# Two attention blocks on one core: every q, k and projection product by quarters, summed in PSUM

## The chip, the cores and the metric

The kernel runs on one core of a Trainium2 chip. The metric is the device time of one launch in microseconds, the median of several runs. TensorE is the engine for matmuls (PE in the profile, PEld its weight loads), VectorE is DVE, ScalarE is ACT, GpSimd is POOL, and SP is the queue from which the transfers are issued.

## The reference

Two layers of self-attention over an image, each with a group norm ahead and a residual sum after it. x has 8 images of 512 channels and 32 x 32 = 1024 tokens, in float32. The layers differ in the group size of the norm and in their weights.

```python
xn = group_norm(x) * gamma + beta
q, k, v = split(einsum('oc,bcn->bon', qkv_w, xn) + qkv_b)   # 8 heads of 64
attn = softmax(einsum('bhdi,bhdj->bhij', q, k) / 8)
out = einsum('bhij,bhdj->bhdi', attn, v)
y = einsum('oc,bcn->bon', proj_w, out) + proj_b + x          # x of the next layer
```

## The kernel before

The work is cut into 16 units (layer, image), one after the other; the result of a unit's first layer goes through HBM (`mid`). In one unit there are four matrix products of 512x512 weights with a 512x1024 input: q, k, v from the normalized x (`xn`), and the projection (`o`) of the attention result (`ao`). Then comes attention. The projection of unit u is done in unit u+1, after that unit's q, k and v, so that it fills TensorE while the softmax's last sums are finished. The order of instructions on every engine is written out by hand; `done`, `rest` and the hooks below hang small work of the other engines behind a given product.

**Products by blocks.** A 512-wide product is cut into 2x2 blocks and done with seven block products instead of eight. Left factors are sums of weight blocks, right factors are sums of input blocks (`mix_weights`, `mix_right`). They are numbered 1 to 7, issued in the order 1, 6, 2, 7, 5, 4, 3, and each result block is a sum of several of them: 1+2; 1+6+5+3; 1+6+7+4; 1+6+7+5. One block product is done in one of two ways:

- whole (`block_product`, L416): four matmuls of 128x128 by 128x512, or eight by 128x256 where the result has tokens in rows (v). The profile counts two records for each float32 matmul.
- by quarters (`inner_products`, L455): the same seven-product scheme once more inside the block, seven matmuls of 128x128 by 128x256. Products 1, 6, 7 and 5 of the seven are copied out of PSUM by ScalarE into SBUF (L460), GpSimd adds them up (`fold`, L468 and L469) and onto the result (`rests`, L647 to L650 and L745).

By quarters go, from the second unit on, q's block products 2, 5, 4, 3, k's 1, 2, 7, 5, 4, 3 and the projection's 2, 3, 4; never v's, and none in the first unit:

```python
INNER = {"q": (2, 5, 4, 3), "k": (1, 2, 7, 5, 4, 3), "o": (2, 3, 4)}
```

PSUM has four pairs of banks, `s0`, `s1`, `a0`, `a1`. Block sums are formed by VectorE from PSUM and an SBUF tile (`p1`, `u2`, `u3` are the partial sums 1, 1+6, 1+6+7). The extra left factors of the quarters (three of 128x128 for each block) are made once per layer, kept in HBM (`inner_left`) and reloaded per unit; the weights themselves stay in SBUF.

**Attention** is 64 steps of two heads each. In a step TensorE makes scores (four matmuls of 64x64 by 64x512, L820) and, one or two steps behind, the product of the exponentials with v (L848). ScalarE takes the exponential into a buffer `p` of `ppool` (four of them, L828), VectorE adds up the softmax sums (L865, L867). `ppool` also holds the residual tiles of the projection. Within the steps the norm of the next unit's x, its right factors and the division by the softmax sums are done. Behind the last step come the last sums (`transposed`, `reduced`) and, in the next unit's first products, `reciprocals`, `divide` (L930) and `bias_last` (L937).

Of the kernel before, what the change touches and what calls it, by code (L numbers as in the profile page):

```python
# [18 lines left out]
P = 128  # L19
# [13 lines left out]
def fast_path(ctx, tc, x, qkv_wT, proj_wT, vecs, groups, out, flag):  # L33
# [5 lines left out]

# [11 lines left out]

    INNER = {"q": (2, 5, 4, 3), "k": (1, 2, 7, 5, 4, 3), "o": (2, 3, 4)}
    assert D == H and C == FD

    def pool(name, bufs, **kw):
# [4 lines left out]
    xnpool = pool("xnpool", 1)  # L69
    aopool = pool("aopool", 1)  # L70
    vpool = pool("vpool", 1)
    qkpool = pool("qkpool", CC)
    ppool = pool("ppool", 4)
    accpool = pool("accpool", 2)
    tpool = pool("tpool", 1)
# [8 lines left out]

# [3 lines left out]

    turns = [t[:, i, :] for i in range(2) for t in (*sbank, *apair)]

    vec = const.tile([P, 2, 6, CC], F32, name="vec")
    gmat = const.tile([P, 2, P], F32, name="gmat")
# [5 lines left out]
    inner_left = [  # L98
        {
            sel: mids.tile([P, len(ks), 3, P], F32, tag=f"il{sel}{l}", name=f"il{sel}{l}")  # L100
            for sel, ks in INNER.items()
# [6 lines left out]

    def gate(*insts):


        n = nc.tensor.nop(nofuse=True)
        n = getattr(n, "ins", n)
        for i in insts:
            tc.add_manual_dep(n, name_of(i), DEP, reason="tiles of the PE run independently")

    def load_x(u, tiles, first=0):
        l, b = units[u]
        src = x[b] if l == 0 else mid[b]
        for c, t in enumerate(tiles, first):  # L120
            nc.sync.dma_start(t, src[c * P : (c + 1) * P, :])

    def load_xn(u):
        t = xnpool.tile([P, CC, N], F32, tag="xn", name=f"xn_{u}")
        load_x(u, [t[:, c, :] for c in range(CC)])
        return t

    def load_res(u):
        tiles = [ppool.tile([P, N], F32, tag="p", name=f"x_{u}_{c}") for c in range(CC)]
        load_x(u, tiles)  # L130
        return tiles

    def load_weights(l, which=range(3), after=None):

        mats = []
        src = qkv_wT[l].rearrange("(c p) o -> p c o", p=P)
        for i in which:
            a = wpool.tile([P, CC, C], F32, tag=f"w{i}", name=f"w{i}_{l}")
            n = nc.sync.dma_start(a, src[:, :, i * C : (i + 1) * C])
            if after is not None:  # L140
                tc.add_manual_dep(
                    getattr(n, "ins", n), name_of(after), DEP, reason="x comes first"
                )
                after = None
            mats.append(a)
        return mats

    def mix_weights(l, mats, engine, first=0):


        lefts, parts = [], []
        add, sub = engine.tensor_add, engine.tensor_sub
        for i, a in enumerate(mats, first):
            a11, a12 = a[:, :2, :FD2], a[:, 2:, :FD2]
            a21, a22 = a[:, :2, FD2:], a[:, 2:, FD2:]
            s1, s2, s4 = (
                wpool.tile([P, 2, FD2], F32, tag=f"s{k}w{i}", name=f"s{k}w{i}_{l}")
                for k in (1, 2, 4)
            )
            parts += [  # L160
                partial(add, s1, a21, a22), partial(sub, s2, s1, a11),
                partial(sub, a21, a11, a21), partial(sub, s4, a12, s2),
            ]
            lefts.append({1: a11, 2: a12, 3: s4, 4: a22, 5: s1, 6: s2, 7: a21})
        return lefts, parts

    def mix_right(name, low, high):


        b11, b12 = low[:, :, :FD], low[:, :, FD:]  # L170
        b21, b22 = high[:, :, :FD], high[:, :, FD:]
        factors = {1: b11, 2: b21, 3: b22, 7: b12}

        def part(i):
            if i == 0:
                for k, n in ((5, 1), (6, 2), (4, 4)):
                    factors[k] = tpool.tile([P, 2, FD], F32, tag=f"{name[0]}{n}", name=f"{name}_t{n}")
            t1, t2, t4 = (factors[k] for k in (5, 6, 4))
            nc.vector.tensor_sub(
                *((t1, b12, b11), (t2, b22, t1), (t4, b21, t2), (b12, b22, b12))[i]  # L180
            )

        return factors, [partial(part, i) for i in range(4)]

    def mix_inner(b, t, engine):


        b11, b12 = b[:, 0, :FD2], b[:, 0, FD2:]
        b21, b22 = b[:, 1, :FD2], b[:, 1, FD2:]
        t1, t2, t3, t4 = (t[:, i, :] for i in range(4))  # L190
        sub = engine.tensor_sub
        return {1: b11, 2: b21, 3: b22, 4: t4, 5: t1, 6: t2, 7: t3}, [
            partial(sub, t1, b12, b11), partial(sub, t2, b22, t1),
            partial(sub, t3, b22, b12), partial(sub, t4, b21, t2),
        ]

    def inner_lefts(k, left, made):
        a11, a12 = left[:, 0, :P], left[:, 1, :P]
        a21, a22 = left[:, 0, P:], left[:, 1, P:]
        s1, s2, s4 = made  # L200
        return {1: a11, 2: a12, 3: s4, 4: a22, 5: s1, 6: s2, 7: a21}

    def mix_inner_in(b, t, engine):

        sub = engine.tensor_sub
        b11, b12 = b[:, 0, :FD2], b[:, 0, FD2:]
        b21, b22 = b[:, 1, :FD2], b[:, 1, FD2:]
        t1, t2, t4 = (t[:, i, :] for i in range(3))
        sub(t1, b12, b11)
        sub(t2, b22, t1)  # L210
        sub(b12, b22, b12)
        sub(t4, b21, t2)
        return {1: b11, 2: b21, 3: b22, 4: t4, 5: t1, 6: t2, 7: b12}

    def mix_inner_left(l, lefts):

        def part(sel, n, k, room, later=None, engine=nc.gpsimd):  # L220
            sub = engine.tensor_sub
            left = lefts[sel][k]
            s1, s2, s4 = room
            a11, a12 = left[:, 0, :P], left[:, 1, :P]
            a21, a22 = left[:, 0, P:], left[:, 1, P:]
            engine.tensor_add(s1, a21, a22)
            sub(s2, s1, a11)
            sub(a21, a11, a21)
            sub(s4, a12, s2)

            def out():
                for j in range(3):
                    nc.sync.dma_start(inner_left[l][sel][:, n, j, :], room[j])

            if later is None:
                out()
            else:
                later.append(out)

        return [partial(part, sel, n, k) for sel in lefts for n, k in enumerate(INNER[sel])]  # L240

    def left_rooms(name, pool, tag, cols):

        t = pool.tile([P, cols], F32, tag=tag, name=name)
        slices = [t[:, i : i + P] for i in range(0, cols, P)]
        return [slices[i : i + 3] for i in range(0, len(slices) - 2, 3)]

    def load_inner_left(u):

        l, _ = units[u]  # L250
        flat = vpool.tile([P, NT, C], F32, tag="v", name=f"il_{u}").rearrange("p t o -> p (t o)")
        made, end = {}, 0
        for sel in "qk":
            ks = INNER[sel]
            first, end = end, end + len(ks) * 3 * P
            part = flat[:, first:end].rearrange("p (k s o) -> p k s o", s=3, o=P)
            nc.sync.dma_start(part, inner_left[l][sel])
            made[sel] = {k: [part[:, j, i, :] for i in range(3)] for j, k in enumerate(ks)}
        return made

    def load_proj(l, tag):
        w = wpool.tile([P, CC, C], F32, tag=tag, name=f"wproj_{l}_{tag}")
        nc.sync.dma_start(w, proj_wT[l].rearrange("(c p) o -> p c o", p=P))
        return w

    def norm_parts(u, xs, lo=0, hi=CC):


        l, _ = units[u]
# [6 lines left out]
        def stats(c, h):  # L276
            if c == lo and h == 0:
                st["stats"] = small.tile([P, CC, NH, 6], F32, tag="stats", name=f"stats_{u}_{lo}")
                st["mv"] = small.tile([P, CC, 2], F32, tag="mv", name=f"mv_{u}_{lo}")[:, :n, :]
            st["last"] = nc.vector.bn_stats(st["stats"][:, c - lo, h, :], xs[:, c, ts(h, FD)])  # L280
# [34 lines left out]

# [16 lines left out]
        def apply(c, h):  # L332
            cols = xs[:, c, ts(h, FD)]
            nc.scalar.activation(  # L334
                cols, cols, AF.Identity,
                bias=st["shift"][:, c - lo : c - lo + 1], scale=st["scale"][:, c - lo : c - lo + 1],
            )

        def apply_now(c, h):
            cols = xs[:, c, ts(h, FD)]  # L340
# [7 lines left out]
    def norm_first(xs, weights, mixing):  # L348

# [4 lines left out]
        ) = (norm_parts(0, xs, lo, lo + 2) for lo in (0, 2))  # L357
# [7 lines left out]
        idle_products(3, xs[:, 0, :])  # L365
# [24 lines left out]
        def rest():  # L390
            variances_2(bank)
            mixing[0]()
# [4 lines left out]
            mixing[1]()  # L397
# [7 lines left out]
    def block_product(bank, a, b, tokens, start, stop, between=None):  # L405
        for i in range(4 if tokens else 2):
            if i == 1 and between is not None:
                between()
# [13 lines left out]
    def blocks(name, left, right, tokens, c11, others, done, u3_in, summed, inner={}, rests=None,  # L422
               u2_in=(trpool, "tr"), between=None, behind=None, p1=None):

# [1056 lines left out]
```

## Time and profile before

| | |
|---|---|
| median of 3 runs | 3257.65 us (3257.36, 3257.65, 3259.85) |
| span of the profiled execution, the only time listed for it | 3256.9 us |
| mean granted clock of TensorE | 0.999 |
| moved by DMA | 192.51 MB, 59 GB/s |

One unit in stages (the fourth), busy microseconds of each engine:

| stage | from, to (us) | length | PE | DVE | ACT | POOL |
|---|---|---|---|---|---|---|
| q | 600.4, 622.8 | 22.4 | 22.4 | 19.8 | 9.6 | 17.7 |
| k | 622.8, 644.6 | 21.8 | 21.8 | 14.9 | 9.3 | 21.5 |
| v | 644.6, 668.8 | 24.2 | 24.2 | 12.9 | 3.6 | 21.3 |
| projection of the unit before | 668.8, 691.7 | 22.9 | 22.9 | 20.8 | 5.1 | 7.1 |
| attention | 691.7, 802.0 | 110.3 | 110.3 | 100.7 | 76.9 | 10.5 |

The span is the time from the first to the last instruction. A run's time also has what lies around it: the median is 0.75 us above the span. A line of the profile names the source line, engine, operation, output and inputs with their shapes, and the number of instructions; in a timeline the first two numbers are start and length in microseconds. The ends of matmuls are modelled, so that a busy PE says that it has work, not that it runs at its peak; the distance from start to start shows its pace.

### The profile page before, as it was taken

Reading aid. Unit: us, or ns where it says so; the run is one execution under the profiler, and the core shown is the slowest. Engines: PE = TensorE matmul, PEld = TensorE weight load, DVE = VectorE, ACT = ScalarE, POOL = GpSimd, SP = SyncE. Lnnn points to the kernel's source line nnn. Section 1 sums busy time; section 2 is a strip of 40 time slices with the busy share of each in tenths; the row PEclk is TensorE's granted clock in tenths of the full one; section 3 lists DMA queues with packets and bytes.
Section 4 is the critical chain, followed back from the end, with each engine's and each line's share of the span. In section 5 each row is a group of like instructions: output and inputs, shape, how many; then the busy total and the mean of one; then the engine's idle time right before and its main releaser. Section 6 shows DMA issues by size and latency. Waiting matters only on the chain.

```text
span 3256.9 us, 56805 instructions
## 1 busy us (share of the span) xinstructions
PE 3244.5 (100%) x22206; PEld 1863.3 (57%) x22206; DVE 2715.3 (83%) x3488; ACT 1650.2 (51%) x2296; POOL 1216.3 (37%) x1207
## 2 busy tenths in 40 slices
PE   9999999999999999999999999999999999999999
PEld 5465474654746547465574655747556474564743
DVE  5887978789787897989979889797897978979786
ACT  1653626546274463744637446373563735637354
POOL 2054171531706317063270732607126071350710
PEclk9999999999999999999999999999999999999999
DMA  3112120121201212023120121201212012120111
GB/s 104 48 45 79 46 79 28 45 79 46 85 22 45 85 43 86 18 71 114 55 87 27 45 86 46 85 16 45 86 46 85 17 54 76 46 85 22 67 71 48
DMA packets 86463, 192.51 MB, mean 59 GB/s; under 512 B 22960, under 2 KB 34992, under 8 KB 84272
## 3 DMA queue, kind: packets, MB, share of 16 engines
q1 hardware_dynamic: 86192, 188.82, 17.0%
q8 instruction: 180, 2.95, 0.4%
q14 instruction: 91, 0.75, 0.1%
HBM read 148.00 MB, written 39.19 MB: 57 GB/s over the span
## 4 chain that ended last, share of the span: by engine, by line
PE 96%; DVE 3%; issue 0%; DMA 0%; ACT 0%; SPq 0%; DVEq 0%
PE a L848 26%; PE s L820 25%; PE s L416 14%; PE a L416 12%; PE a L455 10%; PE s L455 9%; DVE acc L867 1%; PE a L820 1%; PE s L766 0%; PE a L766 0%; DVE tr L880 0%; PE s L361 0%; DVE acc L865 0%; DVE ao L874 0%; DMA xn<-x_dram 0%
## 5 line engine op out<-in xcount | busy, mean ns | idle before, releaser
L828 ACT ACTIVATE p<-s 128x1024 f32<-128x1024 f32 x976 | 998.0, 1024 | 558.0 <-PE s L820 516.6
L848 PE MATMUL a<-p,v 64*64 64x512 f32 x8192 | 1099.8, 589 | 0.0
L820 PE MATMUL s<-q,k 64*64 64x512 f32 x7808 | 1058.1, 590 | 0.0
L867 DVE TENSOR_TENSOR acc<-acc,p 128x1024 f32<-128x1024 f32 x768 | 968.6, 1261 | 61.7 <-ACT p L828 13.0
L848 PEld LDWEIGHTS a<-p,v 64*64 64x64 f32 x8192 | 383.2, 131 | 495.8 <-ACT p L828 350.2
L820 PEld LDWEIGHTS s<-q,k 64*64 64x64 f32 x7808 | 383.5, 133 | 431.9 <-issue 422.8
L1088 POOL TENSOR_TENSOR r<-xn 128x256 f32<-128x256 f32 x30 | 49.5, 1649 | 1175.7 <-DVE acc L867 1038.3
L650 POOL TENSOR_TENSOR k<-k,m_k 128x512 f32<-128x512 f32 x180 | 259.6, 1463 | 0.0
L865 DVE TENSOR_TENSOR acc<-p,p 128x1024 f32<-128x1024 f32 x128 | 156.2, 1220 | 20.5 <-ACT p L828 13.9
L312 POOL TENSOR_TENSOR y<-var,half 128x4 f32<-128x4 f32 (+1 forms) x17 | 33.2, 1950 | 344.4 <-DVE var L310 344.4
L880 DVE STREAM_TRANSPOSE tr<-acc 128x1024 f32<-128x1024 f32 x128 | 157.9, 1234 | 0.0
L650 POOL TENSOR_TENSOR q<-q,m_q 128x512 f32<-128x512 f32 x120 | 157.2, 1325 | 0.0
L890 DVE TENSOR_REDUCE red<-tr 128x32 f32<-128x1024 f32 x128 | 154.4, 1206 | 0.6
L538 DVE TENSOR_TENSOR u_v<-s,p_v 128x1024 f32<-128x1024 f32 x32 | 39.2, 1224 | 123.7 <-PE s L416 123.7
L501 ACT COPY p_o<-a 128x1024 f32<-128x1024 f32 x15 | 15.2, 1012 | 244.2 <-PE a L416 244.2
L874 DVE TENSOR_TENSOR ao<-a,tmp 128x512 f32<-128x512 f32 x128 | 88.0, 688 | 60.9 <-ACT tmp L873 59.6
L460 ACT COPY m_q<-s 128x256 f32<-128x256 f32 x150 | 55.9, 373 | 145.3 <-PE s L455 142.7
L468 POOL TENSOR_TENSOR m_o<-m_o 128x256 f32<-128x256 f32 x45 | 34.2, 760 | 251.7 <-ACT m_o L460 251.7
L416 PE MATMUL s<-x_t,s2w 128*128 128x512 f32 x256 | 117.5, 592 | 0.0
L416 PE MATMUL a<-w,xn 128*128 128x256 f32 x496 | 112.1, 379 | 0.0
L460 ACT COPY m_k<-s 128x256 f32<-128x256 f32 x165 | 61.5, 373 | 93.8 <-PE s L455 90.2
L334 ACT ACTIVATE xn<-xn,shift,scale 128x512 f32<-128x512 f32 x124 | 99.5, 804 | 10.9 <-DVE shift L330 10.9
(291 smaller groups left out, 5130.5 us busy)
## 6 DMA issues: line engine op xcount, KB each, us to landing
rb<-drec SPq DMA_DIRECT2D x128, 256.0 KB, 3.9
xn<-mid SPq DMA_DIRECT2D x36, 512.0 KB, 7.9
il<-ilk SPq DMA_DIRECT2D x15, 1152.0 KB, 7.0
xn<-x_dram SPq DMA_DIRECT2D x32, 512.0 KB, 7.0
x<-x_dram SPq DMA_DIRECT2D x32, 512.0 KB, 5.5
x<-mid SPq DMA_DIRECT2D x28, 512.0 KB, 4.9
il<-ilq SPq DMA_DIRECT2D x15, 768.0 KB, 4.2
mid<-u_o SPq DMA_DIRECT2D x32, 256.0 KB, 2.1
```

What stands on the lines that cost most here:

```text
L334: nc.scalar.activation(cols, cols, AF.Identity, bias=st["shift"][:, c - lo : c - lo + 1], scale=st["scale"][:, c - lo : c - lo + 1],)
L416: nc.tensor.matmul(dst, at[:, c, ts(i, P)], moving[:, c, :], start=start and c == 0 and not (tokens and i % 2), stop=stop and c == 1, skip ...
L455: nc.tensor.matmul(dst[j], a[j], b[j], start=j in (1, 5) or first and j in (2, 4), stop=j not in (1, 6), skip_group_check=True,)
L460: taken.append(nc.scalar.copy(to[j], dst[j]))
L650: w.last[sel].append(add(cols, cols, rest[:, i, :]))
L820: nc.tensor.matmul(bank[e * H : (e + 1) * H, j, :], w.k[pr][j * H : (j + 1) * H, t * P + e * H : t * P + (e + 1) * H], w.q[pr][j * H : (j ...
L828: exp = nc.scalar.activation(p, bank, AF.Exp, scale=SCALE)
L848: nc.tensor.matmul(banks[r][j * H : (j + 1) * H, :], w.v[rows, t, lo : lo + D], p[rows, j, :], start=(t == 0), stop=(t == NT - 1),)
L865: nc.vector.tensor_add(acc, state["first"], p)
L867: nc.vector.tensor_add(acc, acc, p)
L880: nc.vector.transpose(tr, state["acc"].pop(c))
L890: nc.vector.tensor_reduce(red[:, :, qh, :], state["tr"].rearrange("p j (f i) -> p j f i", i=BL), AX.X, ALU.add)
```

## The change

- **All** block products of q, k and projection go by quarters, in every unit; only q's and k's product 1 of the first unit stay whole (`behind`). v stays whole.
- The quarter sums stay in PSUM. Each product has a main pair (`a0` or `a1`) and one pair for help (`s1` or `s0`), taken in turns by `Stream`. Quarter product 1 goes to a helper bank; ScalarE copies it into the main pair as a **seed** (for 1+2); 6 is added to it in the helper bank, copied again (for 1+6+4), then 5, copied twice (for 1+6+5+3 and 1+6+5). Products 2, 4 and 3 are added onto the seeds by TensorE. Product 7 goes to the helper pair's other bank and by ScalarE into an SBUF tile **`late`** (three buffers), which GpSimd adds to the lower half of the result after VectorE has read it (`add_late`). GpSimd's folding goes.
- The end of each product (quarter products 4 and 3) is issued behind the first matmul of the next (`tail`, `close`), in the last one behind the first scores.
- Order of a unit: v, q, k, projection. x's quarter factors are made by GpSimd in v, 16 subtractions. The projection's are made by VectorE in q and k.
- Left factors with their quarter factors are "images" in HBM, seven parts per layer and matrix (896 columns each, v 512); two slots in SBUF receive them product by product: q's and v's during attention, k's and the projection's from the end of v on, 28 loads per unit. First-layer images are made in the first unit, the others by VectorE in the attention of units 0 to 4 (`MAKE`).
- The residual tiles `res` (four, 512 KB each) are loaded during k and projection, and take three of `ppool`'s five buffers at its end, as one is used twice. The residual is added by VectorE at its own pass.

```diff
-    INNER = {"q": (2, 5, 4, 3), "k": (1, 2, 7, 5, 4, 3), "o": (2, 3, 4)}
+    ORDER = (1, 6, 2, 7, 5, 4, 3)
...
-    ppool = pool("ppool", 4)
+    ppool = pool("ppool", 5)
+    latepool = pool("latepool", 3)
...
+        def product(self, a, b, keep, finish):
+            i = self.n % 2
+            self.n += 1
+            main, aux, m, s = apair[i], sbank[1 - i], f"a{i}", f"s{1 - i}"
+            one, seventh = aux[:, 0, :FD2], aux[:, 1, :FD2]
+            q11, q12, q21, q22 = (main[:, r, ts(h, FD2)] for r in range(2) for h in range(2))
...
+            part(1, one, s, 0, True)
+            seed(q11, 0)
+            self.close()
+            part(6, one, s, 0)
+            seed(q21, 1)
+            part(2, q11, m, 0)
+            part(7, seventh, s, 1, not keep)
+            late = latepool.tile([P, FD2], F32, tag="late", name=f"late_{self.n}")
+            on("ACT", nc.scalar.copy(late, seventh), s, 1)
+            part(5, one, s, 0)
+            seed(q12, 0)
+            def tail():
+                part(4, q21, m, 1)
+                seed(q22, 1)
+                part(3, q12, m, 0)
+                finish(main, m, late)
+            self.tail = tail
...
+    def add_late(t, late):
+        cols = in_two(t[:, 1, :])
+        return nc.gpsimd.tensor_add(cols, cols, twice(late))
...
+        def u2(main, m, late):
+            t = st["u2"] = accpool.tile([P, 2, FD], F32, tag="acc", name=f"u2_{name}")
+            on("DVE", nc.vector.tensor_add(t, main, st["p1"]), m, 0, 1)
+            add_late(t, late)
...
+        def fifth(main, m, late):
+            wide(main, m)
+            result(1, 1, "u3")(main, m, late)
...
+        def third(*args):
+            take(0, 1, *args)
+            more(1, 0, "u3")
+            store(1, 0)
+            more(0, 1, "u2")
+            store(0, 1)
...
+    MAKE = {0: (0, "o"), 1: (1, "v"), 2: (1, "q"), 3: (1, "k"), 4: (1, "o")}
...
+            at("q", 1, partial(o_rooms, True), partial(ro.mix, 3))
+            at("q", 6, partial(ro.mix, 2))
+            at("q", 2, o_part((5, 6), 0, 1))
+            at("q", 7, o_part((5, 6), 2, 3))
+            at("q", 4, o_part((1, 7), 0, 1))
+            at("q", 3, o_part((1, 7), 2, 3))
+            at("k", 2, partial(o_rooms, False), o_part((4,), 0, 1, 2, 3))
+            at("k", 4, o_part((2, 3), 0, 1))
+            at("k", 3, o_part((2, 3), 2, 3))
...
+            at("q", 1, *(partial(load_image, l, "k", 0, k) for k in ORDER))
+            for k in ORDER:
+                at("q", k, partial(load_image, lo, "o", 1, k))
...
+            at("o", 3, partial(stats_of, 6, 7))
```

`at("q", 2, ...)` hangs work behind q's block product 2; an `o_part` step is one subtraction of 128x512 by VectorE. `fifth` is product 5, with two passes of VectorE over the main pair: `wide` adds it to `u2`, `result` adds `u3` to it. `third` is the projection's last product: `take` adds the main pair onto `res` and hangs `add_late` behind it, `more` adds a partial sum from SBUF.

## The prediction

> **What bounds the kernel now.** I read the busy times, then the chain, then TensorE's own waits, then its timeline.
>
> ```profile
> span 3256.9 us, 56805 instructions
> PE 3244.5 (100%) x22206; PEld 1863.3 (57%) x22206; DVE 2715.3 (83%) x3488; ACT 1650.2 (51%) x2296; POOL 1216.3 (37%) x1207
> PE 96%; DVE 3%; issue 0%; DMA 0%; ACT 0%; SPq 0%; DVEq 0%
> ```
> The end is set by TensorE (96% of the chain), and its four lines of waits over the whole span come to 5.9 us, 4.5 of them the first load. So TensorE is not merely busy: it has no gap. A change pays only by taking matmuls away, and every new wait is paid in full.
>
> The timeline of TensorE in one unit (start, us, instructions) prices the two kinds of product:
> ```profile
> 675.67 0.59 PE L455 MATMUL s<-ao,wproj_wproj 128*128 128x256 f32 x2
> ...
> 678.69 3.60 PE L416 MATMUL s<-ao,wproj_wproj 128*128 128x512 f32 x8
> 682.12 3.60 PE L416 MATMUL a<-o_t,s1w 128*128 128x512 f32 x8
> ```
> A product by quarters takes 678.69 - 675.67 = 3.02 us (seven matmuls, 0.4317 apart), a whole one 682.12 - 678.69 = 3.43. The gain is 0.41 each. The v product (16 records, 644.63 to 648.08) takes 3.45 and stays. A unit lasts 201.58 us (600.38 to 801.96).
>
> Next, the loop that a quarter product lives in, from the mixed timeline:
> ```profile
> 613.80 0.59 PE L455 MATMUL s<-x_t,s1w 128*128 128x256 f32 x2
> 614.44 0.37 ACT L460 COPY m_q<-s 128x256 f32<-128x256 f32 x1 [2.32 <-PE s L455]
> 614.92 0.37 PEld L455 LDWEIGHTS s<-r,il 128*128 128x128 f32 x2
> 615.10 0.59 PE L455 MATMUL s<-r,il 128*128 128x256 f32 x2
> ```
> The copy starts 0.64 after its matmul's start and ends at 614.81; the matmul that overwrites the copied bank loads its weights 0.11 later and starts 0.29 after that end. With two matmuls between (3 x 0.4317 = 1.295 us) the loop 0.64 + 0.37 + 0.29 = 1.30 just closes: that weight load came 0.46 after the one before instead of 0.43. Two matmuls hide a copy with nothing to spare.
>
> Last, VectorE beside GpSimd, from the same timeline:
> ```profile
> 622.73 1.02 DVE L636 TENSOR_TENSOR q<-a,u_q 128x512 f32<-128x512 f32 x2
> 623.39 1.26 POOL L650 TENSOR_TENSOR q<-q,m_q 128x512 f32<-128x512 f32 x1
> 623.67 1.27 DVE L578 TENSOR_TENSOR k<-xn 128x256 f32<-128x256 f32 x1
> 624.61 0.91 POOL L647 TENSOR_TENSOR q<-u_q,m_q 128x256 f32<-128x256 f32 x1
> 624.97 0.83 DVE L578 TENSOR_TENSOR k<-xn,k 128x256 f32<-128x256 f32 x1
> ```
> L636 reads PSUM (a) and is not slowed. L578 reads SBUF twice: 1.27 us where L209, the same shape with GpSimd idle, takes 0.43. It waited until GpSimd's addition was over, and then GpSimd's next one waited for it: they take turns.
>
> **What the Trainium skill says.** "SBUF — State Buffer", Who interferes with whom: an instruction of VectorE with two SBUF inputs and a GpSimd one that reads SBUF exclude each other for their whole length; with at most one SBUF input VectorE doesn't contend. The lines above agree (1.27 against 0.43). "PSUM — Partial Sum Buffer", PSUM bank collisions: accesses of two engines to one bank must be ordered even on different columns; hence the new copies wait by bank. No run here shows a collision. "ScalarE: Activation LUTs", Step-by-step: ScalarE's writes to PSUM have a lower latency than to SBUF; no copy of before writes PSUM, so no trace here shows it.
>
> **The change part by part.**
>
> *Removed from TensorE.* Of q, k and projection, 13 of 21 products per unit go by quarters now (4, 6, 3), all 21 afterwards: 8 x 15 units. In the first unit 12 of its 14 q and k products, none before. (120 + 12) x 0.41 = **54.1 us saved**.
>
> *Copies on ScalarE.* 4 per quarter product become 5 (four seeds within PSUM, one `late`): 780 become (15 x 21 + 12) x 5 = 1635, at 0.37 some 315 us more beside TensorE. Three seeds per product are on TensorE's path (after 1 for 6, after 6 for 5, after 5 for 3), each with two matmuls between. A seed of 0.37 or less costs nothing. Bounds: shorter gains nothing, as the loop is closed already; 0.03 longer costs 327 x 3 x 0.03 = 29 us. I take 0.
>
> *The main pair is reused two products later.* VectorE may start when product 3 is through and the last seed done: 9 x 0.4317 + 0.64, some 4.57 us after the product's first matmul. The seed of the next but one is due at 14 x 0.4317 + 0.64 = 6.68. About 2.1 us are left, 2.0 with a hand-over of 0.1. One pass over PSUM (128x1024, L538: 1.22) or two halves (1.41) fit; product 5 has two passes, 1.14 + 1.22 = 2.36 from start to end, so they end at 6.93, and the seed and with it matmul 6 come 0.25 late. That is three times per unit, twice in the first; q's is part of the next item, k's and projection's are 30 x 0.25 = 7.5, the first unit's 0.5.
>
> *VectorE's projection factors in q.* After q's products 2 and 7 two 128x512 subtractions from SBUF are queued behind the result, while GpSimd's `late` addition (1.25) becomes ready under the first. They alternate: 1.14 (result) + 0.61 + 1.2 (GpSimd) + 0.61 = 3.6 against a period of 3.02; then 1.32 + 0.61 + 1.2 + 0.61 = 3.7. Product 5 starts 0.6 + 0.7 = 1.3 late; 0.25 of its own is added, and about as much of slack was there before: **1.3 us per unit** (0.25 if VectorE goes twice running, 1.9 at the most), x 15 = 19.5.
>
> *Entry to attention.* The second scores take the bank of the last product's copies and must wait for its last seed: matmul 4 + 0.64 + 0.37 + 0.29 = 1.30 where 0.86 is free: 0.4 x 16 = 6.4. Behind the last product VectorE now has result, two additions into `res` (the second waits for GpSimd's 1.25) and two statistics before the first softmax sum: 1.14 + 1.14 + 1.3 + 1.14 + 1.2 = 5.9 us from 1.9 after the first scores. The sum ends 9.1 after them; before it started 3.2 after them (694.88 against 691.70). The fourth exponential needs that p buffer (`res` holds three of five); exponential 1.02 + 0.29 puts product 3 at 10.4, where 9.0 was due: **1.5 per unit** (0.5 without GpSimd in the way, 2.5 if the additions drag), x 15 = 22.5.
>
> *Mixing left factors in five units' attention.* Up to eight VectorE passes of 128x896, about 1.0 each by VectorE's rate in L538, in chunks of 13.7 us with 11.1 to 13.3 us busy in the stage view. The backlog is some 2 us at the end, and v's product 4 is late by most of it: it is due 17.27 after v's start and needs VectorE's pass over product 7, which I put at an end of 16.2 (the last softmax sum 3.3 after the stage's start as now, then evacuation, transposition, reduction, four passes and the reciprocals, 10.7, and some 2.2 of turns with GpSimd). 0.8 to spare, 1.6 x 5 units: 8 us (0 to 15).
>
> *Moved, at nothing.* v first: attention's last evacuation and v's sums have 3.45 per product. GpSimd's 16 subtractions of x (12 x 1.25 + 4 x 0.72 = 18 us) fit into v's 24, uncovered they would hold q's first matmuls. SP's queue gets 28 image loads per unit, 11.5 MB: k and projection 6.4 MB, free to start from v's middle; at the o stage's rate (212 GB/s at a share of 0.53, so 400 at full) 16 us, and k needs them only when q (21 us) is over. Behind them queue the reloads of x, due two to four products later. If they were late, each microsecond would be k's. The new opening (v, q, k first products instead of q, k, v) has the same three products before the first product 6: 0, within 2.
>
> Sum: -54.1 + 19.5 + 8.0 + 6.4 + 22.5 + 8 = **+10.3**. Against the profiled span of 3256.9 this is 3267.2; the runs' median is 0.75 above that span, which makes 3268.
>
> **Rivals.** *Alternation is mild (faster).* If VectorE gets its pair of subtractions through before GpSimd, product 5 in q costs 0.25 and the entry 0.4 + 0.5: 15 x 1.6 + 0.9 = 25, mixing 0: 3257.65 - 54.1 + 25 = 3229. For it: GpSimd's work halves, from 78 us per unit to about 40. Against it: the turns at 623 to 626. It decides once VectorE's second pass of q's product 5 ends within 2.0 us of being due.
> *Seeds in PSUM are slower.* 0.03 us over the closed loop, three times in 327 products: +29 on the forecast, 3297. For it: no spare in 614.44 to 615.10. Against: the skill's remark.
> *Everything hides.* 3257.65 - 54.1 = 3204. Against it: two passes in 2.0 us.
>
> **How the numbers follow.** Forecast 0.42 (own range 3250 to 3284), mild 0.33 (3212 to 3240), slow seeds 0.20 (3284 to 3315), all hidden 0.05. The range 3215 to 3305 leaves out all hidden, the low edge of mild and the top of slow seeds, under 0.2. A measurement can tell 0.2% (6.5 us) from no change: faster 0.38 (mild, hidden), same 0.15 (forecast's lower part), slower 0.47.
>
> **What would show it.** TensorE's waits should no longer be empty: matmuls on ScalarE's seeds, one of over 1 us per unit in q, about 0.25 in k and projection, one of about 1.5 on an exponential in the first steps of attention. The first softmax sum should start near 8 us after the first scores. q's subtractions should show 1 to 1.9 us instead of 0.69. Wrong it is if the sums of those waits are under 1.8 us a unit (mild), or if most products show three short waits (slow seeds), or if TensorE waits on DMA.

## The result and the profile after

The changed kernel takes 3298.94 us (median of 4 runs, 3297.93 to 3299.36), the kernel before 3257.77 in runs beside it: a ratio of 1.0125 (95% interval 1.0111 to 1.0139), 41 us slower. It lies within the stated range, but 31 us above the predicted time. The profiled execution has a span of 3296.1 us, 39.2 above the 3256.9 of before.

The page of the changed kernel, busy times and shares of the chain:

```profile
span 3296.1 us, 59529 instructions
PE 3221.7 (98%) x22998; PEld 2083.2 (63%) x22998; DVE 2900.7 (88%) x3298; ACT 1888.6 (57%) x3077; POOL 889.7 (27%) x559
PE 70%; DVE 21%; issue 5%; ACT 2%; DMA 1%; SPq 0%; POOL 0%; DVEq 0%; ACTq 0%
```

TensorE was all of the chain but 4%; now VectorE has a fifth of it. GpSimd's busy time fell by 327 us (from 1216.3), and yet, as the timelines further down show, GpSimd is what VectorE waits for. TensorE's waits over the whole span (who waited for whom: us in total, times, longest), 5.9 us before:

```profile
PE s L398 <- DVE u_v L625: 35.0, 15, 4.5
PE s L421 <- ACT a L426: 13.6, 16, 0.9
PE a L733 <- ACT p L713: 8.6, 6, 2.6
...
PE s L703 <- ACT a L426: 2.6, 16, 0.2
```

The second, third and last line are the forecast's: q's late seed, the exponential at the entry, the second scores. The first, the largest, was forecast only for five units, and for another product: it comes once in every unit after the first. L398 is v; the wait is that of v's fourth product in the order, 7, which is added onto the banks that VectorE's pass L625 (`u2`, the sum with product 6) must read first. TensorE's timeline at the start of an ordinary unit, the seventh (unit 6; units are counted from 0 below):

```profile
1240.31 3.62 PE L398 MATMUL a<-w,xn 128*128 128x256 f32 x16
1245.73 3.72 PE L398 MATMUL s<-w,xn 128*128 128x256 f32 x16 [1.81 <-DVE u_v L625]
```

Product 7 should start 3.45 after product 2, at 1243.76; it starts 1.97 later. VectorE's timeline ahead of it:

```profile
1228.13 1.22 DVE L217 TENSOR_TENSOR xt<-xn,xt 128x1024 f32<-128x1024 f32 x1
1229.26 2.29 DVE L752 TENSOR_TENSOR acc<-acc,p 128x1024 f32<-128x1024 f32 x1
1231.48 2.29 DVE L812 SCALAR_TENSOR_TENSOR ao<-ao,rb 128x1024 f32<-128x1024 f32 x1
...
1233.70 6.70 DVE L752 TENSOR_TENSOR acc<-acc,p 128x1024 f32<-128x1024 f32 x3
...
1242.19 1.22 DVE L772 TENSOR_REDUCE red<-tr 128x32 f32<-128x1024 f32 x1
1243.33 1.22 DVE L217 TENSOR_TENSOR xn<-xn 128x1024 f32<-128x1024 f32 x1
1244.46 1.22 DVE L625 TENSOR_TENSOR u_v<-s,p_v 128x1024 f32<-128x1024 f32 x1
```

Up to 1229 a pass of 128x1024 takes 1.22 (pace 1.13); the next five take 2.23 each (6.70 for three). Then GpSimd's timeline, same kernel:

```profile
1228.35 2.13 POOL L933 TENSOR_TENSOR xa<-xn 128x512 f32<-128x512 f32 x1 [77.48 <-PE s L703]
1230.55 2.14 POOL L933 TENSOR_TENSOR xa<-xn,xa 128x512 f32<-128x512 f32 x1
1232.77 2.14 POOL L933 TENSOR_TENSOR xb<-xn,xa 128x512 f32<-128x512 f32 x1
1234.86 2.25 POOL L933 TENSOR_TENSOR k<-xt 128x512 f32<-128x512 f32 x1
1237.19 4.34 POOL L933 TENSOR_TENSOR k<-xt,k 128x512 f32<-128x512 f32 x2
```

A piece alone takes 1.25, so these records include waiting. Start plus length gives their ends, and the ends of the two engines alternate: GpSimd 1230.48, VectorE 1231.55, GpSimd 1232.69, VectorE 1233.77. Each ends about one piece of work (1.1) after the other: turns, as in the prediction's lines at 623 to 626, but in a place where I had not looked for them. The six x pieces hang behind v's products 1 and 6, but nothing holds them until then: they start 5 us before v, under the last softmax sums. The same stretch of the kernel before:

```profile
595.23 1.22 DVE L179 TENSOR_TENSOR x_t<-xn,x_t 128x1024 f32<-128x1024 f32 x1
596.37 1.22 DVE L867 TENSOR_TENSOR acc<-acc,p 128x1024 f32<-128x1024 f32 x1
597.50 1.22 DVE L930 SCALAR_TENSOR_TENSOR ao<-ao,rb 128x1024 f32<-128x1024 f32 x1
...
598.64 5.08 DVE L867 TENSOR_TENSOR acc<-acc,p 128x1024 f32<-128x1024 f32 x3
...
605.51 1.22 DVE L890 TENSOR_REDUCE red<-tr 128x32 f32<-128x1024 f32 x1
```

There only three passes ran beside GpSimd, at 1.69 each, since its pieces were of 128x256. The reduction ended 11.5 us after the mixing line (L179) had started, in the changed kernel 15.3 (from L217 to the end of L772).

### The profile page after: what moved, and what is told of

The parts are those of the page before. It is cut to its first block, busy times and chain, and to the rows that moved or that the text cites. A ratio compares the mean times of both kernels' runs of the same rounds, so it can differ in the third digit from the quotient of the medians.

```text
span 3296.1 us, 59529 instructions
## 1 busy us (share of the span) xinstructions
PE 3221.7 (98%) x22998; PEld 2083.2 (63%) x22998; DVE 2900.7 (88%) x3298; ACT 1888.6 (57%) x3077; POOL 889.7 (27%) x559
## 4 chain that ended last, share of the span: by engine, by line
PE 70%; DVE 21%; issue 5%; ACT 2%; DMA 1%; SPq 0%; POOL 0%; DVEq 0%; ACTq 0%
PE s L703 18%; PE a L733 17%; PE s L421 17%; PE a L421 12%; DVE acc L752 9%; PE s L398 2%; PE a L398 2%; DVE tr L764 2%; DVE acc L750 2%; DVE ao L759 1%; ACT p L713 1%; DMA lt<-red 1%; DVE red L772 1%; DVE tot L793 1%; PE a L703 1%
## 5 line engine op out<-in xcount | busy, mean ns | idle before, releaser
L713 ACT ACTIVATE p<-s 128x1024 f32<-128x1024 f32 x976 | 1000.3, 1025 | 528.1 <-PE s L703 446.5
L426 ACT COPY a<-s 128x256 f32<-128x256 f32 x1308 | 463.3, 357 | 302.0 <-PE s L421 184.4
L438 ACT COPY late<-s 128x256 f32<-128x256 f32 x327 | 121.8, 373 | 178.7 <-PE s L421 178.7
L819 ACT ACTIVATE ao<-ao,vec 128x512 f32<-128x512 f32 x128 | 88.3, 714 | 221.9 <-DVE ao L812 221.9
L398 PE MATMUL a<-w,xn 128*128 128x256 f32 x768 | 178.2, 381 | 0.0
L398 PEld LDWEIGHTS a<-w,xn 128*128 128x128 f32 x768 | 144.4, 190 | 31.7 <-issue 12.2
L772 DVE TENSOR_REDUCE red<-tr 128x32 f32<-128x1024 f32 x128 | 154.2, 1205 | 0.6
L750 DVE TENSOR_TENSOR acc<-p,p 128x1024 f32<-128x1024 f32 x128 | 152.4, 1190 | 1.0 <-ACT p L713 1.0
L421 PE MATMUL s<-k,w 128*128 128x256 f32 x492 | 146.3, 379 | 0.0
L421 PE MATMUL a<-xn,w 128*128 128x256 f32 x492 | 146.3, 379 | 0.0
L421 PE MATMUL s<-xn,w 128*128 128x256 f32 x492 | 146.3, 379 | 0.0
L421 PE MATMUL a<-xt,w 128*128 128x256 f32 x462 | 139.0, 382 | 0.0
L421 PE MATMUL s<-xt,w 128*128 128x256 f32 x432 | 128.5, 379 | 0.0
L458 POOL TENSOR_TENSOR res<-res,late 128x512 f32<-128x512 f32 x60 | 103.6, 1726 | 88.4 <-DVE res L546 88.4
```

What stands on the lines that cost most here:

```text
L398: step()
L421: nc.tensor.matmul(dst, a[j], b[j], start=start, stop=j != 1, skip_group_check=True),
L426: n = nc.scalar.copy(dst, one)
L438: on("ACT", nc.scalar.copy(late, seventh), s, 1)
L458: return nc.gpsimd.tensor_add(cols, cols, twice(late))
L713: exp = nc.scalar.activation(p, bank, AF.Exp, scale=SCALE)
```

## The experiments

All were run beside the kernel before, whose median was 3258.1 and 3259.0 us in the two sets. The changed kernel was not run again in these sets; its 3299 us is taken from the section above. "Loss" is the distance between starts on TensorE beyond the usual one, from the trace; the "restart" is 0.10 us more between the first matmul after a wait and the next.

**GpSimd's pieces later.** The pieces that need VectorE's last mixing come first from the second unit on, so that GpSimd cannot start ahead of it (lines that stay the same are left out):

```diff
-        at("v", 1, make_rooms, partial(right.mix, 3), part_of((2, 3), 0, 1, 2))
...
-        at("v", 2, partial(right.mix, 2), part_of((1, 7), 0, 1, 2))
...
+        if u:
+            at("v", 1, make_rooms, partial(right.mix, 3), part_of((1, 7), 0, 1, 2))
...
+            at("v", 2, partial(right.mix, 2), part_of((2, 3), 0, 1, 2))
...
```

> From the second unit on GpSimd takes its x pieces in another order: the four that need v's last mixing of xn come first, so that GpSimd starts only when VectorE is through with the end of attention. Theory one (taking turns): in the changed kernel TensorE loses 2.45 us in v in ordinary units and some 5 in three others, 46 us in all, because VectorE's sums, each 1.14 us alone, last 2.2 beside GpSimd's subtractions. Without that VectorE's pass over v's product 6 ends 3.8 us earlier, before it is due: v loses under 0.4 us per unit and the kernel takes 3253 to 3265 us. Rival (VectorE simply has too much to do before that pass, since v is first now): the pass stays late, v loses over 1.5 us per unit, 3285 us or more. Second rival: GpSimd's pieces are late for q's first products, a new wait on GpSimd of over 1 us per unit.

Measured: 3252.87 us, ratio to before 0.9982 (0.9975 to 0.9989): 46 us off the changed kernel. Its VectorE timeline, same place of the same unit:

```profile
1216.36 1.22 DVE L772 TENSOR_REDUCE red<-tr 128x32 f32<-128x1024 f32 x1
1217.50 1.22 DVE L217 TENSOR_TENSOR xn<-xn 128x1024 f32<-128x1024 f32 x1
1219.73 1.22 DVE L625 TENSOR_TENSOR u_v<-s,p_v 128x1024 f32<-128x1024 f32 x1 [1.02 <-PE s L398]
```

v starts at 1212.45; VectorE is ready 6.3 us later and now waits for TensorE's product 6 itself. v's loss fell from 2.55 to 0.10 us in ordinary units. No new wait on GpSimd came instead, and the rival (VectorE has too much to do before that pass) is refuted. With this one reordering the change is 5 us faster than the kernel before.

**Smaller pieces in the old place.** Order unchanged, each piece of 128x512 made by two of 128x256:

```diff
-            sub = engine.tensor_sub
+            def sub(out, a, b):
+                n = out.shape[1] if engine is nc.gpsimd else 1
+                for i in range(n):
+                    at = slice(i, i + 1) if n > 1 else slice(None)
+                    engine.tensor_sub(out[:, at], a[:, at], b[:, at])
```

> GpSimd's x subtractions stay where they are, but each of 128x512 is made by two of 128x256: more instructions, the same data. If the two engines take whole turns, a sum of VectorE's waits for a piece half as long: 1.7 us each, as in the kernel before (5.08 us for three), where the changed kernel shows 2.23. Five such passes lie ahead of VectorE's pass over v's product 6, which then ends 2.7 us earlier: v's loss of 2.45 us per unit falls to under 0.5, and the kernel takes 3262 to 3272 us. If instead the two share a port evenly, the size of a piece changes nothing and the time stays at 3299.

Measured: 3257.09 us, ratio 0.9996 (0.9987 to 1.0005), 42 us off. VectorE's timeline:

```profile
1211.60 1.75 DVE L757 TENSOR_TENSOR acc<-acc,p 128x1024 f32<-128x1024 f32 x1
1213.27 1.75 DVE L817 SCALAR_TENSOR_TENSOR ao<-ao,rb 128x1024 f32<-128x1024 f32 x1
...
1214.95 5.07 DVE L757 TENSOR_TENSOR acc<-acc,p 128x1024 f32<-128x1024 f32 x3
```

1.69 each, as in the kernel before. GpSimd has the same data to go through in more instructions, and VectorE's five passes are 2.7 us sooner: each pays for about one GpSimd piece, long or short. By the expectation an even sharing of a port would have left 2.23. The pass of `u2` now ends 9.9 us after v's start, just ahead of its due time of 10.35, and v's loss is 0.10 us in ordinary units, under the 0.5 expected; hence the gain above the expected one.

**Fewer subtractions before product 5 of q.**

```diff
-            at("q", 7, o_part((5, 6), 2, 3))
+            at("k", 6, o_part((5, 6), 2, 3))
```

> Two of the four subtractions of projection factors that VectorE does behind q's product 7 are moved behind k's product 6. Theory (turns with GpSimd behind product 7 make product 5's two passes late): q's wait of 1.16 us per unit falls to k's and projection's 0.19, 15 us in all, 3284 us. Rival (product 5's two passes are late by themselves, or by the pair behind product 2): the wait stays over 0.8 us, 3294 us or more. Rival two: the pair is late for projection's product 6, or delays k's passes; then a new wait in k or projection takes the gain back.

Measured: 3286.48 us, ratio 1.0088 (1.0071 to 1.0105): 12.5 us off. In the changed kernel VectorE's second pass of product 5 came at 1277.93, behind the two subtractions (L990), of which the second is shown:

```profile
1275.12 1.75 DVE L990 TENSOR_TENSOR ot<-ot 128x512 f32<-128x512 f32 x1
1276.80 1.21 DVE L496 TENSOR_TENSOR u_q<-a,u_q 128x1024 f32<-128x1024 f32 x1
1277.93 1.21 DVE L509 TENSOR_TENSOR q<-a,u_q 128x1024 f32<-128x1024 f32 x1
```

The next seed came after it, and TensorE 1.06 late, as its timeline shows; the last line is behind the restart:

```profile
1278.15 0.59 PE L421 MATMUL a<-xt,w 128*128 128x256 f32 x2
1279.64 0.70 PE L421 MATMUL s<-xa,w 128*128 128x256 f32 x2 [0.90 <-ACT a L426]
1280.18 0.59 PE L421 MATMUL a<-xn,w 128*128 128x256 f32 x2
```

The same place with the edit:

```profile
1275.48 0.59 PE L421 MATMUL a<-xt,w 128*128 128x256 f32 x2
1276.00 0.70 PE L421 MATMUL s<-xa,w 128*128 128x256 f32 x2
1276.54 0.59 PE L421 MATMUL a<-xn,w 128*128 128x256 f32 x2
```

0.09 late plus a restart of 0.10, as in k and projection. The loss of q fell by 0.97 us per unit, 14.5 in all; some of it came back as longer waits in v (36.2 us in place of 35.0) and on the exponential (9.2 in place of 8.6). With the pair behind product 7 away, the pair behind product 2 costs nothing, as VectorE is then idle for 1.22 us ahead of product 5. While both stood it had a part: in the changed kernel VectorE goes from the first pair into product 7's pass at 1273.21 without a pause, some 0.5 after that product's last seed (1272.71), and from there into the second pair and product 5. So some 0.5 of the 1.16 may be the first pair's; moving that one alone was not tried.

**Raw loads later.** The raw left factors that units 0 to 4 mix are loaded at step 4 of attention, counted from 0, instead of before it.

```diff
-            load_raw(*make, left_slots[0])
...
+            if make is not None and s == 4:
+                load_raw(*make, left_slots[0])
```

> In the five units whose attention mixes a left factor the raw loads are issued at the fifth step of attention instead of ahead of its first. Theory (the loads share the DMA engines with the stores that the fourth exponential waits for: 5.7 us for a store of 256 KB there, 2.7 in other units): the wait of 1.4 us on the exponential goes in the units 1 to 4, 3293 us. Rival (the wait is VectorE's, the first softmax sum comes late): it stays, 3299 us. v's waits are unchanged in either.

Measured: 3294.17 us, ratio 1.0113 (1.0096 to 1.0129). The times alone don't tell 5 us from nothing, the trace does: the waits on the exponential (L713) fell from 8.6 us (6) to 3.9 (2). Those in units 1, 2, 4 and 14 are gone; the first unit's 2.6 stays, and so do 1.3 in unit 3. Unit 14 mixes nothing, so the 1.5 us there are not the edit's. ScalarE's timeline of the changed kernel at the entry of unit 2, from the third exponential on (the fourth and fifth are merged):

```profile
500.90 1.02 ACT L713 ACTIVATE p<-a 128x1024 f32<-128x1024 f32 x1
505.93 2.05 ACT L713 ACTIVATE p<-s 128x1024 f32<-128x1024 f32 x2 [4.01 <-DVE acc L750]
```

The same with the edit, third, fourth and fifth:

```profile
497.90 1.02 ACT L713 ACTIVATE p<-a 128x1024 f32<-128x1024 f32 x1
500.98 1.02 ACT L713 ACTIVATE p<-s 128x1024 f32<-128x1024 f32 x1 [2.07 <-DMA mid<-res]
502.92 1.03 ACT L713 ACTIVATE p<-s 128x1024 f32<-128x1024 f32 x1 [0.91 <-DVE acc L750]
```

Both theories are half right. The fourth exponential did wait for the first softmax sum (L750), as the forecast and the rival have it, not for a store. But with the edit, as in most of the changed kernel's other units, it takes the buffer of a stored residual tile instead, 3.1 us after the third and not 5.0, and the fifth takes the sum's. The store was late in unit 2 of the changed kernel: it landed 8.2 us after the first exponential had started (506.85 against 498.61), 5.7 us from its issue instead of 2.7, while the DMA share was 1.01 from 500 to 505 with the four raw loads in flight (a residual tile is 512 KB, not the 256 of the expectation). That this lateness is why the sum's buffer was taken is not shown. It doesn't look like a choice made as the kernel runs: in unit 14 the fourth exponential waited for the store until 2956.10, though the sum's buffer was free at 2955.81. And a store can be late without the loads: in unit 3 with the edit they are issued behind all stores, at 709.28, when the store issued at 706.48 would have landed after 2.7 us; it took 4.8, and the fourth exponential started at 711.34.

**First scores behind matmul 4.**

```diff
+        def open(self):
+            self.fourth()
+            self.early = True
...
             if s == 0:
                 before += w.last["q"] + w.last["k"]
+                close.__self__.open()
```

`fourth` is matmul 4 with its seed, taken out of `tail`; `open` issues it ahead of the scores, and `tail` then leaves it out.

> The first scores are issued behind the last product's matmul 4 instead of ahead of it, so that matmul 4's seed has two other blocks of matmuls in front of the second scores. Theory (the second scores wait for that last seed): the two gaps of 0.44 and 0.16 us around the entry to attention go, 0.4 to 0.6 us in each of 16 units: 3290 to 3293 us. Rival (the entry is set by VectorE or by the exponential that frees the bank): unchanged within 2 us.

Measured: 3296.06 us, ratio 1.0115 (1.0098 to 1.0132), 3 us below the changed kernel, whose interval (1.0111 to 1.0139) overlaps with it. In the trace the waits of the second scores on ScalarE (2.6 us) are gone and 0.23 us per entry with them, 3.7 in all; a third of a microsecond stays as the switch from scores to matmul 3 and the restart. The theory holds for less than was expected.

**Seeds in two halves.**

```diff
-                n = nc.scalar.copy(dst, one)
-                on("ACT", n, m, bank)
-                on("ACT", n, s, 0)
+                for c in range(2):
+                    n = nc.scalar.copy(dst[:, ts(c, P)], one[:, ts(c, P)])
+                    on("ACT", n, m, bank)
+                    on("ACT", n, s, 0)
```

> Every seed on ScalarE is made by two copies of 128x128 instead of one of 128x256: the same data, one fixed part more. If the loop of copy and matmul is closed with nothing to spare, as the forecast assumed, each of three seeds in 327 products pays what the pair lasts beyond 0.37 us: at 0.2 to 0.25 us each, 0.1 us or so, +60 to +150 us. If there is slack of 0.1 us or more in the loop, the time stays within 10 us of the changed kernel's 3299.

Measured: 3337.67 us (one run), 39 above the changed kernel: between the two expectations. The timeline:

```profile
1292.07 0.61 PE L421 MATMUL s<-xr,w 128*128 128x256 f32 x2
...
1292.72 0.53 ACT L427 COPY a<-s 128x128 f32<-128x128 f32 x2 [0.34 <-PE s L421]
...
1293.30 0.30 PEld L421 LDWEIGHTS s<-xr,w 128*128 128x128 f32 x2 [0.16 <-ACT a L427]
1293.38 0.62 PE L421 MATMUL s<-xr,w 128*128 128x256 f32 x2
```

The pair of copies takes 0.53 instead of 0.37, and the matmul that waits for it starts 0.13 after its end, not 0.29. The loop is 1.31 us, hardly more than its room of 1.295. With one copy it is 1.15: 0.14 us to spare. TensorE does slow down, by 0.024 us at nine in ten of the 981 seeds on its path, 21 us in all. Another 8 are 30 matmuls in k and the projection that came 0.28 late; the rest lies in v and at the entry to attention.

**The edits together.** The three edits of GpSimd's order, q's subtractions and raw loads in one kernel, and then the first scores as well.

> The three edits together: GpSimd's x pieces later, two of the projection factors' subtractions behind k's product 6, the raw loads at the fifth step. If their causes are separate their gains add: 46 + 12.5 + 5 us off the changed kernel's 3299, 3235 us, which is faster than before. If one wait covered another, less: 3245 or more.

> The same and the first scores behind matmul 4: another 6 to 9 us, 3226 to 3230 us; with all waits gone the forecast's saving of 54 us would give 3204, and what is left above that are the starts and restarts of TensorE and the first unit.

Measured: 3233.93 us, ratio 0.9928 (0.9911 to 0.9944), and 3232.71 us, ratio 0.9920 (0.9903 to 0.9936). The gains of three causes add up (65 us off the changed kernel where 64 were expected): they are separate. The fourth can't be told from nothing here. Both versions beat the kernel before, by 25 and 26 us. Two lines of TensorE's waits with the three edits, what is left of the exponential and of v:

```profile
PE a L733 <- ACT p L713: 5.5, 4, 2.6
...
PE s L398 <- DVE u_v L632: 2.0, 4, 0.8
```

## Why the prediction was right in range and 31 us short

Term by term, in us; the measured side is TensorE's loss in the changed kernel's trace. The last term is what the kernel before lost by itself and the changed one does not: 28 restarts in its products by quarters, and 0.8 and 1.0 us in two units.

| term | forecast | measured |
|---|---|---|
| 132 products by quarters | -54.1 | -54.1, the pace held |
| q: turns with GpSimd, product 5 | 19.5 | 15 x 1.16 = 17.4 |
| k and projection, product 5 | 7.5 | 30 x 0.19 = 5.7 |
| entry, second scores | 6.4 | 15 x 0.57 = 8.6 |
| entry, fourth exponential | 22.5 | 4 x 1.4 + 1.6 = 7.2 |
| mixing in five units | 8 | 3 x 3.8 + 4.4 + 4 x 0.4 = 17.4 |
| v in every unit | 0 | 15 x 2.45 = 36.8 |
| first unit, products and entry | 0.5 | 3.8 |
| lost by the kernel before itself | 0 | -4.6 |
| sum | +10.3 | +38.2 (span: +39.2) |

For v 2.45 is taken and not 2.55, as the restart of 0.10 behind attention was there before the change too, at q's first matmul (0.53 against 0.43).

**Right: the saving.** The pace held with the seeds in PSUM. In the changed kernel a matmul into the helper bank, the copy of its sum and the next matmul into the same bank read

```profile
1275.56 0.59 PE L421 MATMUL s<-xr,w 128*128 128x256 f32 x2
...
1276.19 0.36 ACT L426 COPY a<-s 128x256 f32<-128x256 f32 x1 [0.45 <-PE s L421]
...
1276.85 0.59 PE L421 MATMUL s<-xr,w 128*128 128x256 f32 x2
```

1.29 us apart, which is three times 0.43. So 54.1 us were indeed taken away, and some 93 added. The rival "seeds in PSUM are slower" fails: the seeds show no short waits, and the experiment with seeds in two halves shows room. The forecast's reason, "the loop is closed already", was wrong by 0.14 us: I took the hand-over of 0.29 in one place, where the matmul was on pace and not waiting for the copy, for the shortest one.

**Right: q, k, projection.** The two subtractions behind product 7, their turn with GpSimd and the late seed of product 5 were there at nearly the forecast size, 1.16 against 1.3; how much of it the pair behind product 2 adds, for which the working charged 0.6, was not measured by itself. In k and projection 0.19 was lost where 0.25 was forecast, of which the restart is 0.10. The working has a slip of 0.04 there: 9 x 0.4317 + 0.64 is 4.53, not 4.57.

**Wrong: v at nothing.** The step that failed is "Moved, at nothing": GpSimd's 18 us were compared with v's 24 us, and not with what VectorE does when they start. The working for the mixing units then took "the last softmax sum 3.3 after the stage's start as now". It ended 7.1 after it (1233.70 + 6.70 against 1233.30), because five passes now waited for pieces of 128x512 instead of three for 128x256. And the first pass that meets a deadline is `u2` behind product 6, due 10.35 after v's start, not the pass over product 7, due 17.27, that I checked. Both experiments on it give nearly all of this back: with the pieces moved, v's loss in the 15 units behind the first falls from 50 us to 4, with the pieces cut to 10, units with mixing included.

**Right in price, wrong in number: the exponential.** Where the fourth exponential takes the first sum's buffer, in units 1 to 4, it costs 1.4 us (1.5 forecast), and the sum started 8.1 us after the first scores even in other units (1332.36 against 1324.25), as stated. But the step "the fourth exponential needs that `p` buffer" holds in these units alone. In the ten after them it takes a store's buffer, ready 2 us earlier, and TensorE loses nothing except in unit 14 (1.6 us), where that store took 4.9 us; why is left open. In the last unit it takes the sum's again, at a loss of 0.2. The working took one order of buffers for all 15 units.

**Too low: the mixing.** It was forecast at 8 us (0 to 15) and at v's product 4; it cost 17.4, most of it at product 7. There units 3 to 5 lose 3.8 us more than others. Their waits are some 2.5 longer, and then TensorE itself goes slower, which the working did not have. In unit 3:

```profile
625.19 5.36 PE L398 MATMUL s<-w,xn 128*128 128x256 f32 x16 [4.45 <-DVE u_v L625]
630.39 3.62 PE L398 MATMUL a<-w,xt 128*128 128x256 f32 x16
```

This product takes 5.20 us and not 3.45. Its first matmul records are 0.427 apart instead of 0.216, and the profile gives a mean granted clock of 0.68 from 625.19 to 630.39. Units 4 and 5 show the same. With GpSimd's pieces moved the three units lose only 0.9, 0.6 and 1.5 in v, at full clock. Units 1 to 4 lose another 0.4 each in attention, where the norm's small matmuls wait for VectorE.

In the first unit the mixing takes another way, ScalarE's queue. ScalarE's timeline of the changed kernel there reads

```profile
145.49 0.81 ACT L309 ACTIVATE xn<-xn,shift,scale 128x512 f32<-128x512 f32 x1 [2.65 <-DVE shift L305]
146.21 1.00 ACT L713 ACTIVATE p<-s 128x1024 f32<-128x1024 f32 x1
```

that is, the norm's scaling of the next x stands ahead of an exponential on ScalarE and waits for VectorE's small norm steps, which stand behind a mixing pass of 1.08. The profile books it as a wait on the exponential, 2.6 us; behind it, too, matmuls go at half their pace for 3.4 us, which makes 4.4 in all. Neither part of the mixing was tried by itself.

The Trainium skill, "SBUF — State Buffer", Who interferes with whom, says that two SBUF inputs on VectorE exclude a reading GpSimd. The prediction cited it for q and didn't ask where else the two engines meet. The traces agree. In the kernel before, the reduction of one SBUF input (L890 at 605.51) takes its 1.22 while GpSimd is at work, and neither is slowed:

```profile
605.77 0.73 POOL L1088 TENSOR_TENSOR r<-x_t 128x256 f32<-128x256 f32 x1
```

The sums of two SBUF inputs ahead of it are slowed, and GpSimd's pieces beside them take 1.6 to 1.7.

## What to carry to other kernels

When work is moved to GpSimd, list VectorE's instructions with two SBUF inputs in the stretch where it **can** start (by its data, not by where it stands in the source), and add one GpSimd piece to each of them; then look for the first pass of VectorE with a deadline behind them. Long GpSimd pieces are cheap for GpSimd (1.25 us against 2 x 0.72 here) and dear for VectorE: cut them, or give them an input that is made late. A saving on a packed engine is real only if every queue that hands buffers to it keeps its slack; here three small placements cost more than 132 shorter products gave.

## What the runs showed of the hardware

- A VectorE pass of 1.14 us with two SBUF inputs takes 1.69 beside a running GpSimd with pieces of 128x256 and 2.23 with 128x512: 0.55 and 1.09 more, some 0.16 less than such a piece takes alone (0.72 and 1.25).
- A ScalarE copy within PSUM, 128x256, takes 0.36 us (mean 357 ns), hardly less than the one to SBUF (373 ns). With split seeds TensorE's waiting matmul starts 0.13 us after the copy's end, behind the longer wait in q 0.05 after it, with the restart to follow.
- After the waits of 0.9 and 1.8 us in q and v TensorE's first matmul record takes 0.10 us longer than its pace (0.32 against 0.216 to the next start).
- After the three waits of 4.1 to 4.5 us in the changed kernel TensorE's records come 0.427 us apart for 3.4 us (granted clock 0.51 from 625.19 to 628.60 in unit 3). After 2.6 us in the first unit they did so here and with GpSimd's pieces moved, but not with the three edits together; after the 1.8 us of ordinary units in no run.
